# A channel's way back from its spectra, woven into the next channel's work (one Trainium2 core, four-block image network, channel stage)

## The chip, the cores and the metric

One core of one Trainium2 chip runs the whole program in one launch. The metric is device time in microseconds; lower is better. The kernel before took 14596.81 us (median of three runs, 14577.73 to 14602.56). Its profiled execution took 14588.21 us.

## What is computed

The reference applies four residual blocks to x (32 images, 192 channels, 56 x 56 pixels), each to a group-normalised input (32 groups of six channels):

```
x = x + L0(_gn(x), ...)    # agent attention
x = x + L1(_gn(x), ...)    # a recurrence over the pixels in both directions
x = x + L2(_gn(x), ...)    # every channel shifted by whole pixels, then blurred by 3 x 3 taps
x = x + L3(_gn(x), ...)    # a 55 x 55 convolution of every channel, by FFT
```

The last two are what the changed part computes. For L3:

```
xf = jnp.fft.rfft2(x, s)
kf = jnp.fft.rfft2(k[0], s)
y = jnp.fft.irfft2(xf * kf[None], s)
y = y[..., Kh // 2:Kh // 2 + H, Kw // 2:Kw // 2 + W]
return y + bias * x
```

The group norm between L2 and L3 needs the mean and the variance of six whole channels before any of the six can be convolved.

## The kernel before

The program has four stages in a row: `make_filter` (the filter's spectra), `attention` (L0), `scan_pairs` (L1) and `channel_blocks` (L2 and L3). Only `channel_blocks` is touched. It fills the last 30% of the span.

It works channel by channel, with all 32 images of a channel in one tile of 114 partitions (two images of 56 rows, each with a row of means) by 16 image pairs by 56 columns. Channels go in groups of GROUP = 6, which are the norm's groups. A group passes through these helpers:

- `shift(q, j)`, once for each channel. It loads x (L1477), multiplies it by a row matrix (16 TensorE instructions in two batches of PSUM, L1484; VectorE scales and evicts each to `turned`, L1491), then by a column matrix (L1501), adds the result to x (L1509) and sums x (L1510). `matrices` makes the two matrices for four channels at a time on GpSimd; one of them passes through TensorE (L1446) and VectorE (L1448).
- `middle(q)`: the group's mean, six small matmuls (L1517) and a copy (L1522).
- `centre(q, j)`, once for each channel: x less the mean into a padded tile (VectorE, L1526), its squares (ScalarE, L1528) and their sums (VectorE, L1529).
- `spread(q)`: 1 / sqrt of the variance, six matmuls (L1517) and two ScalarE instructions (L1534, L1535).
- `convolve(q, j)`, once for each channel, in five steps that depend on each other. **Row spectra**: 16 TensorE instructions (eight float32 matmuls, each recorded as two instructions) into three PSUM tiles (L1627), evicted by 12 ScalarE copies to `y` (L1633). **Column spectra**: for three batches of 5, 5 and 6 image pairs a real and an imaginary matmul (L1547, into the PSUM tiles `re` and `im`). **Products** with the filter's spectrum: six VectorE instructions a batch (L1554 to L1560), which leave `real` and `imag`. **Way back along one axis**: 32 matmuls (64 instructions, L1567) into four PSUM tiles, each evicted by ScalarE to `z` (L1574). **Way back along the other**: four matmuls (eight instructions, L1583) into two PSUM tiles, which VectorE scales (L1585) and adds to x (L1586). Two DMAs then store x (L1588).

The driving loop pairs the groups. While group n is shifted and centred, group n - 1 is convolved, one channel for each j: at j = 0, 1, 2 two channels of group n are shifted and one of group n - 1 convolved ("shift channels" below), at j = 3, 4, 5 two are centred and one convolved ("centre channels"). The first group has nothing to convolve beside it and the last nothing to shift.

What sets the order of instructions on an engine: the Tile framework's scheduler. It takes the program's order as the priority and moves an instruction ahead where its own model finds an earlier one not ready. Each engine then executes its list in that order, with semaphores between the engines. As built, each shift channel's TensorE list holds both shifts in full, then the row spectra, the column spectra and both ways back of one channel. Only the seams overlap: the first batches' way back (L1567) stands among the last batch's column spectra (L1547).

Pools: `d_x` has 15 tiles x, `d_w` two of each work tile (`y`, `real`, `imag`, `z`, `turned` and the rest). PSUM's eight banks are four `ps` tiles, two `re` and two `im`. The four `ps` tiles serve L1484, L1501, L1627, L1567, L1583, L1517 and L1446 alike.

Of the kernel before, what the change touches and what calls it, by code (L numbers as in the profile page):

```python
# [20 lines left out]
F32 = mybir.dt.float32  # L21
# [24 lines left out]
GROUP = C // 32  # L46
# [1314 lines left out]
def channel_blocks(ctx: ExitStack, tc: tile.TileContext, a, k, x2, rs2, spectra, out):  # L1361
# [10 lines left out]
    NI, NG = NB // 2, NB // 4  # L1372
# [3 lines left out]
    wp = ctx.enter_context(tc.tile_pool(name="d_w", bufs=2))  # L1376
# [51 lines left out]
    def matrices(n):  # L1428

        if n in made:  # L1430
            return made[n]
        got = []
        for d, diff in ((1, diff_y), (0, diff_x)):
            r, m = diff.shape
            t = [wp.tile([r, m], F32, name=f"tap{d}{f}", tag=f"tap{d}{f}", bufs=1) for f in range(3)]
            for f in range(3):
                i = 2 * n + d
                nc.gpsimd.tensor_scalar(
                    t[f], diff, where[:r, i, f : f + 1], gs[:r, i, f : f + 1], ALU.is_equal, ALU.mult
                )  # L1440
            mat = wp.tile([r, m], F32, name=f"mat{d}", tag=f"mat{d}", bufs=3)
            nc.gpsimd.tensor_tensor(t[0], t[0], t[1], ALU.add)
            nc.gpsimd.tensor_tensor(mat, t[0], t[2], ALU.add)
            if d == 1:
                ps = pp.tile([128, BANK], F32, name="ps", tag="ps", bufs=4)
                nc.tensor.matmul(ps[:PR, :PR], lags, mat, start=True, stop=True)  # L1446
                mat = wp.tile([r, m], F32, name="mat2", tag="mat2", bufs=3)
                nc.vector.tensor_copy(mat, ps[:PR, :PR])  # L1448
            got.append(mat)
        made.clear()  # L1450
        made[n] = got
        return got
# [18 lines left out]
        return q  # L1471

    def shift(q, j):
        c = q.n * GROUP + j
        rows, cols = matrices(c // 4)
        x = xp.tile([PR, NI, S], F32, name="x", tag="x")
        nc.sync.dma_start(out=x, in_=x2[c].rearrange("s h g w -> (s h) g w"))  # L1477
        flat = x.rearrange("p g w -> p (g w)")
        turned = wp.tile([2 * S, NG, 2, S + 1], F32, name="turned", tag="turned")
        for g0 in range(0, NG, 4):  # L1480
            n = min(4, NG - g0)
            ps = psum()
            for g in range(n):
                nc.tensor.matmul(  # L1484
                    ps[: 2 * S, g * PR : (g + 1) * PR],
                    flat[:, (g0 + g) * 2 * S : (g0 + g + 1) * 2 * S],
                    rows,
                    start=True,
                    stop=True,
                )  # L1490
            nc.vector.tensor_tensor(  # L1491
                turned[:, g0 : g0 + n].rearrange("p g s h -> p (g s) h"),
                ps[: 2 * S, : n * PR].rearrange("p (g h) -> p g h", h=S + 1),
                _bc(q.scale[:, j, g0 : g0 + n].rearrange("p g s -> p (g s)"), [2 * S, 2 * n, S + 1]),
                ALU.mult,
            )
        for g0 in range(0, NG, 4):
            n = min(4, NG - g0)
            ps = psum()
            for g in range(n):  # L1500
                nc.tensor.matmul(  # L1501
                    ps[:PR, g * 2 * S : (g + 1) * 2 * S],
                    turned[:, g0 + g].rearrange("p s h -> p (s h)"),
                    cols,
                    start=True,
                    stop=True,
                )
            xc = flat[:, g0 * 2 * S : (g0 + n) * 2 * S]
            nc.vector.tensor_tensor(xc, xc, ps[:PR, : n * 2 * S], ALU.add)  # L1509
        nc.vector.tensor_reduce(q.sums[:, 0, j, :], x, AX.X, ALU.add)  # L1510
        q.x.append(x)

    def means(q, i):

# [5 lines left out]
    def middle(q):  # L1520
        q.mean = sp.tile([PR, NI], F32, name="mean", tag="mean")
        nc.vector.tensor_copy(q.mean, means(q, 0))  # L1522

    def centre(q, j):
        t = padded[(q.n * GROUP + j) % len(padded)]
        nc.vector.tensor_tensor(t[:, :, 0:S], q.x[j], _bc(q.mean, [PR, NI, S]), ALU.subtract)  # L1526
        sq = wp.tile([PR, NI, S], F32, name="sq", tag="sq")
        nc.scalar.activation(sq, t[:, :, 0:S], AF.Square)  # L1528
        nc.vector.tensor_reduce(q.sums[:, 1, j, :], sq, AX.X, ALU.add)  # L1529
        q.padded.append(t)  # L1530
# [3 lines left out]
        nc.scalar.activation(q.rs, means(q, 1), AF.Ln, bias=eps)  # L1534
        nc.scalar.activation(q.rs, q.rs, AF.Exp, scale=-0.5)  # L1535

    def convolve(q, j):
        c = q.n * GROUP + j
        y = wp.tile([128, NI, 2, 42], F32, name="y", tag="y")
        _rows_to_spectra(nc, psum, q.padded[j], f1, y, NG)  # L1540
        real, imag = (wp.tile([84, NI, 2, 42], F32, name=n, tag=n) for n in ("real", "imag"))
        gr, gi = (q.g[:, j, i, :].unsqueeze(1) for i in range(2))
        for i0, n in _batches(NI):
            f = []
            for i, name in enumerate(("re", "im")):
                ps = pp.tile([84, BANK], F32, name=name, tag=name)
                nc.tensor.matmul(  # L1547
                    ps[:, : n * 84], f2[:, i, :], y[:, i0 : i0 + n].rearrange("p g s u -> p (g s u)"), start=True, stop=True
                )
                f.append(ps[:, : n * 84].rearrange("p (g u) -> p g u", u=42))  # L1550
            shape = [84, 2 * n, 42]
            a0, a1 = (wp.tile([84, 12, 42], F32, name=m, tag=m)[:, : 2 * n] for m in ("a0", "a1"))
            to = [t[:, i0 : i0 + n].rearrange("p g s u -> p (g s) u") for t in (real, imag)]
            nc.vector.tensor_tensor(a0, f[0], gr.to_broadcast(shape), ALU.mult)  # L1554
            nc.vector.tensor_tensor(a1, f[1], gi.to_broadcast(shape), ALU.mult)  # L1555
            nc.vector.tensor_tensor(to[0], a0, a1, ALU.subtract)  # L1556
            a0, a1 = (wp.tile([84, 12, 42], F32, name=m, tag=m)[:, : 2 * n] for m in ("a2", "a3"))
            nc.vector.tensor_tensor(a0, f[0], gi.to_broadcast(shape), ALU.mult)  # L1558
            nc.vector.tensor_tensor(a1, f[1], gr.to_broadcast(shape), ALU.mult)  # L1559
            nc.vector.tensor_tensor(to[1], a0, a1, ALU.add)  # L1560
        z = wp.tile([84, NI, 2, S], F32, name="z", tag="z")
        for i0 in range(0, NI, 4):
            n = min(4, NI - i0)
            ps = psum()
            for i in range(n):
                for m, part in enumerate((real, imag)):
                    nc.tensor.matmul(  # L1567
                        ps[:84, i * 2 * S : (i + 1) * 2 * S],
                        part[:, i0 + i].rearrange("p s u -> p (s u)"),
                        f3[:, m, :],  # L1570
                        start=(m == 0),
                        stop=(m == 1),
                    )
            nc.scalar.copy(  # L1574
                z[:, i0 : i0 + n].rearrange("p g m w -> p (g m w)"), ps[:84, : n * 2 * S]
            )
        x = q.x[j]
        for i0 in range(0, NI, 8):
            n = min(8, NI - i0)
            ps = psum()  # L1580
            got = ps[:PR, : n * S].rearrange("p (g w) -> p g w", w=S)
            for m in range(2):
                nc.tensor.matmul(got, f4[:, m, :], z[:, i0 : i0 + n, m, :], start=(m == 0), stop=(m == 1))  # L1583
            o = wp.tile([PR, 8, S], F32, name="o", tag="o")[:, :n]
            nc.vector.tensor_tensor(o, got, _bc(q.rs[:, i0 : i0 + n], [PR, n, S]), ALU.mult)  # L1585
            nc.vector.tensor_tensor(x[:, i0 : i0 + n], x[:, i0 : i0 + n], o, ALU.add)  # L1586
        for s in range(2):
            nc.sync.dma_start(  # L1588
                out=out[s::2, c].rearrange("b h w -> h b w"), in_=x[(S + 1) * s : (S + 1) * s + S]
            )  # L1590

    before = None
    for n in range(C // GROUP + 1):
        q = begin(n) if n < C // GROUP else None
        for j in range(GROUP):
            if q is not None:
                if j < 3:
                    shift(q, 2 * j)
                    shift(q, 2 * j + 1)
                else:  # L1600
                    if j == 3:
                        middle(q)
                    centre(q, 2 * j - 6)
                    centre(q, 2 * j - 5)
            if before is not None:
                convolve(before, j)
        if q is not None:
            spread(q)
        before = q


def _batches(n):
# [93 lines left out]
```

## Time and profile before

| | |
|---|---|
| median of three runs | 14596.81 us |
| profiled execution | 14588.21 us, of which the span is 14586.4 us |
| mean granted TensorE clock over the span | 0.927 |
| first store of the channel stage (L1588) | at 10065.4 us |
| the group means (L1522), 32 of them | from 10025.6 us to 14409.0 us |
| channel stage, 10127 to 14409 us (4282 us): TensorE busy | 3848.15 us, clock 0.98 |
| the same: VectorE busy | 3186.79 us |
| the same: ScalarE busy | 1284.45 us |

The page lists busy times, groups of instructions and DMA issues for the whole program. The channel stage has to be read from windows of the trace: the share of each engine there, the list of waits (engine and line, what it waited for, total, number, longest), and the timeline, in which each row is a start, a duration, an engine, a line, and in brackets the engine's idle time before it with what ended it.

### The profile page before, as it was taken

The numbers are of one execution on the slowest core, as the hardware profiler recorded it, in microseconds if no ns is written. First come the engines' busy times: TensorE is split into PE (matmuls) and PEld (weight loads), VectorE is DVE, ScalarE is ACT, GpSimd is POOL, SyncE is SP. The second block draws the span as 40 slices with busy tenths as digits, with TensorE's granted clock in tenths as the row PEclk, the third lists the DMA queues.
The fourth block names the chain that finished last, engine by engine and source line by source line (L and its number), as shares of the span: only waits on it lengthen the run. The fifth ranks groups of instructions, "written<-read, shape, count | busy, mean of one in ns | idle before, by whom it ended". The sixth has DMA issues, their size and how long they took to land. (4 is left out here: it accounts for less than half of the span.)

```text
span 14586.4 us, 164705 instructions
## 1 busy us (share of the span) xinstructions
PE 12276.2 (84%) x63542; PEld 7620.1 (52%) x63542; DVE 11320.3 (78%) x15929; ACT 5972.2 (41%) x10826; POOL 2178.7 (15%) x2238
## 2 busy tenths in 40 slices
PE   4999999999999976777677677767899889988898
PEld 2655655655565553333333333335666666666666
DVE  4878877887887878878887887886777777777777
ACT  2444444444444434444444444443323232323323
POOL 0000000000000004434443443442000000000000
PEclk8999999999999988888888888888999999999999
DMA  2001001000100112232223222322111111111111
GB/s 54 27 27 40 27 27 40 27 27 32 35 27 27 40 53 66 60 71 71 65 67 81 66 60 68 75 51 56 35 37 36 37 37 36 37 35 38 36 37 23
DMA packets 886784, 654.14 MB, mean 45 GB/s; under 512 B 764942, under 2 KB 772857, under 8 KB 876976
## 3 DMA queue, kind: packets, MB, share of 16 engines
q1 hardware_dynamic: 885992, 643.51, 16.7%
q8 instruction: 505, 8.27, 0.2%
q14 instruction: 287, 2.35, 0.1%
HBM read 402.88 MB, written 240.50 MB: 44 GB/s over the span
## 5 line engine op out<-in xcount | busy, mean ns | idle before, releaser
L587 DVE SCALAR_TENSOR_TENSOR o<-v_a,dww,o 128x896 f32<-128x896 f32 (+1 forms) x1024 | 1052.8, 1028 | 390.1 <-ACT v_a L561 282.7
L1633 ACT COPY y<-ps 64x252 f32<-64x252 f32 (+1 forms) x2376 | 807.6, 340 | 1298.6 <-PE ps L1627 1266.4
L1567 PE MATMUL ps<-f,imag 84*84 84x112 f32 x6144 | 1032.0, 261 | 130.2 <-DVE imag L1560 128.5
L1574 ACT COPY z<-ps 84x448 f32<-84x448 f32 x768 | 405.3, 528 | 1771.1 <-PE ps L1567 1771.1
L1567 PE MATMUL ps<-f,real 84*84 84x112 f32 x6144 | 1035.7, 261 | 1.7
L1567 PEld LDWEIGHTS ps<-f,imag 84*84 84x84 f32 x6144 | 744.0, 153 | 275.6 <-DVE imag L1560 206.4
L1567 PEld LDWEIGHTS ps<-f,real 84*84 84x84 f32 x6144 | 748.8, 153 | 160.1 <-issue 68.6
L1041 ACT ACTIVATE q<-q 128x784 f32<-128x784 f32 x384 | 329.3, 858 | 1225.4 <-DVE q L1036 1223.9
L1035 POOL COPY c<-p 128x1 f32<-128x1 f32 x384 | 696.2, 1813 | 665.3 <-DVE p L1034 611.8
L1048 POOL MEMSET c<- 128x1 f32 x192 | 18.3, 99 | 5182.8 <-PE ps L719 5172.1
L1034 DVE TENSOR_TENSOR_SCAN q<-decay,c,ek 128x784 f32<-128x784 f32 x384 | 702.0, 1832 | 105.3 <-ACT ek L1064 105.2
L1583 PE MATMUL ps<-z,f 84*114 84x448 f32 x1536 | 658.5, 551 | 129.5 <-ACT z L1574 129.5
L604 ACT ACTIVATE pr<-ps,low 98x896 f32<-98x896 f32 (+1 forms) x384 | 350.1, 914 | 1015.4 <-DVE low L602 1015.4
L1585 DVE TENSOR_TENSOR o<-ps,rs 114x448 f32<-114x448 f32 x384 | 239.5, 624 | 631.7 <-PE ps L1583 630.5
L1035 POOL COPY c<-q 128x1 f32<-128x1 f32 x384 | 483.1, 1258 | 1460.7 <-DVE q L1034 1390.3
L1034 DVE TENSOR_TENSOR_SCAN p<-decay,c,bv 128x784 f32<-128x784 f32 x384 | 699.9, 1833 | 0.0
L674 PE MATMUL ps<-gq_a,xs_a 128*112 128x294 f32 x1792 | 643.7, 442 | 0.0
L600 PE MATMUL ps<-xs_a,gk_a 128*98 128x448 f32 (+1 forms) x1536 | 639.0, 497 | 0.0
L587 DVE SCALAR_TENSOR_TENSOR o<-v_c,dww,o 128x448 f32<-128x448 f32 (+1 forms) x1024 | 634.0, 619 | 4.0
L1547 PE MATMUL re<-y,f 128*84 128x420 f32 (+1 forms) x1152 | 561.5, 569 | 84.8 <-ACT y L1633 74.8
L601 PE MATMUL ps<-xs_c,gk_c 125*98 125x448 f32 (+1 forms) x1536 | 631.6, 492 | 0.0
L675 PE MATMUL ps<-gq_c,xs_c 125*112 125x294 f32 x1792 | 627.7, 433 | 0.0
(352 smaller groups left out, 29243.6 us busy)
## 6 DMA issues: line engine op xcount, KB each, us to landing
x<-x SPq DMA_DIRECT2D x512, 392.0 KB
x<-x SPq DMA_DIRECT2D x512, 196.0 KB
x<-x SPq DMA_DIRECT2D x192, 399.0 KB
out_x<-x SPq DMA_DIRECT2D x384, 196.0 KB
x_a<-in_x SPq DMA_DIRECT2D x32, 1568.0 KB
x<-x_a SPq DMA_DIRECT2D x32, 1568.0 KB
x_c<-in_x SPq DMA_DIRECT2D x64, 392.0 KB
x<-x_c SPq DMA_DIRECT2D x64, 392.0 KB
```

The costliest lines, as they stand in the source:

```text
L587: nc.vector.scalar_tensor_tensor(dst, tap(i), dww[:, t, i : i + 1], dst, ALU.mult, ALU.add)
L600: mm(ps[P2, h, :n], g[:, cols], xs_a[j][:, px], start=True, stop=False)
L601: mm(ps[P2, h, :n], gk_c[0:KC, 2 * j + h, cols], xs_c[j][0:KC, px], start=False, stop=True)
L674: mm(ps[:SUB, i, :HA], xs_a[j][:, px], g, start=True, stop=False)
L675: mm(ps[:SUB, i, :HA], xs_c[j][0:KC, px], gq_c[0:KC, 2 * j + (q + i) // ns], start=False, stop=True)
L1034: nc.vector.tensor_tensor_scan(out, decay[:, of(t)].to_broadcast([128, MC]), data, at, ALU.mult, ALU.add)
L1035: nc.gpsimd.tensor_copy(at, s[:, last : last + 1])
L1547: nc.tensor.matmul(ps[:, : n * 84], f2[:, i, :], y[:, i0 : i0 + n].rearrange("p g s u -> p (g s u)"), start=True, stop=True)
L1567: nc.tensor.matmul(ps[:84, i * 2 * S : (i + 1) * 2 * S], part[:, i0 + i].rearrange("p s u -> p (s u)"), f3[:, m, :], start=(m == 0), stop= ...
L1574: nc.scalar.copy(z[:, i0 : i0 + n].rearrange("p g m w -> p (g m w)"), ps[:84, : n * 2 * S])
L1583: nc.tensor.matmul(got, f4[:, m, :], z[:, i0 : i0 + n, m, :], start=(m == 0), stop=(m == 1))
L1633: nc.scalar.copy(y[64 * m : 64 * m + 64, 2 * g0 + i : 2 * (g0 + n) : 2], got[64 * i : 64 * i + 64, :, :, m, :])
```

## The change

`convolve` is cut in two, and all helpers become generators that yield between steps. `analyse` holds the row spectra, the column spectra and the products; `synthesise` holds both ways back, the addition to x and the stores. The driving loop runs `synthesise` of a channel one turn later, beside the next channel's `analyse`, and takes the steps of four generators in turn: the analysis (`taking`), two shifts or centres (`two`), and the previous channel's way back (`ending`). `middle` moves into the first `centres`. No instruction is added, removed or changed in size; pools and tiles are the same.

```
-    def convolve(q, j):
-        c = q.n * GROUP + j
+    def analyse(q, j):
+
         y = wp.tile([128, NI, 2, 42], F32, name="y", tag="y")
         _rows_to_spectra(nc, psum, q.padded[j], f1, y, NG)
-        real, imag = (wp.tile([84, NI, 2, 42], F32, name=n, tag=n) for n in ("real", "imag"))
+        yield
+        real, imag = q.product = [wp.tile([84, NI, 2, 42], F32, name=n, tag=n) for n in ("real", "imag")]
...
             nc.vector.tensor_tensor(to[1], a0, a1, ALU.add)
+            yield
+
+    def synthesise(q, j, product):
+
+        c = q.n * GROUP + j
+        real, imag = product
         z = wp.tile([84, NI, 2, S], F32, name="z", tag="z")
...
+            yield
         x = q.x[j]
...
             nc.vector.tensor_tensor(x[:, i0 : i0 + n], x[:, i0 : i0 + n], o, ALU.add)
+            yield
...
-    before = None
+    def centres(q, j):
+
+        if j == 0:
+            middle(q)
+        centre(q, j)
+        yield
+        yield
+
+    before, ending = None, iter(())
     for n in range(C // GROUP + 1):
         q = begin(n) if n < C // GROUP else None
         for j in range(GROUP):
+            two = [iter(()), iter(())]
             if q is not None:
-                if j < 3:
-                    shift(q, 2 * j)
-                    shift(q, 2 * j + 1)
-                else:
-                    if j == 3:
-                        middle(q)
-                    centre(q, 2 * j - 6)
-                    centre(q, 2 * j - 5)
-            if before is not None:
-                convolve(before, j)
+                two = [shift(q, 2 * j + i) if j < 3 else centres(q, 2 * j - 6 + i) for i in range(2)]
+            taking = analyse(before, j) if before is not None else iter(())
+            for step in (
+                taking, two[0], two[0], taking, ending, ending, two[0], taking, ending, ending, two[1], two[1], taking,
+                ending, two[1], ending,
+            ):
+                next(step, None)
+            for rest in (*two, taking, ending):
+                for _ in rest:
+                    pass
+            ending = synthesise(before, j, before.product) if before is not None else iter(())
         if q is not None:
             spread(q)
         before = q
+    for _ in ending:
+        pass
```

`shift` yields after its row pass and after its column pass, and otherwise stays as it was. The scheduler still stands between this order and the chip. As built, TensorE's list for a shift channel c is: row spectra of c, row pass of one shift, column pass with the first column spectra of c among it, half the way back of c - 1 (L1567 before), the second column spectra, the other half, the second shift's two passes with the third column spectra among them, L1583 of c - 1. A centre channel has the same without the shifts.

More of the change, by code (lines that the diff above doesn't have):

```diff
@@ L1590, in convolve @@
             )
-    before = None
+    def centres(q, j):
+        if j == 0:
+            middle(q)
+        centre(q, j)
+        yield
+        yield
+    before, ending = None, iter(())
     for n in range(C // GROUP + 1):
```

## Prediction

> **What bounds the kernel now.** The page first: TensorE has the largest share of the whole span.
>
> ```profile
> PE 12276.2 (84%) x63542; PEld 7620.1 (52%) x63542; DVE 11320.3 (78%) x15929; ACT 5972.2 (41%) x10826; POOL 2178.7 (15%) x2238
> ```
>
> That is an average over four stages. The window from the group of means at 10127 us to the last mean at 14409 us is the changed stage alone (busy times in the order PE, PEld, DVE, ACT, POOL, then granted clock, DMA share, GB/s):
>
> ```profile
> 10127.00:14409.00 4282.00, 3848.15 (x24547) 2831.01 (x24546) 3186.79 (x5284) 1284.45 (x3105) 264.67 (x410) 0.98 0.14 36
> ```
>
> TensorE is busy 90%, VectorE 74%, ScalarE 30%, DMA 14%. So TensorE is the bound, with holes. Who makes the holes is in the waits of 10600 to 14586 us (total, times, longest):
>
> ```profile
> PE ps L1583 <- ACT z L1574: 113.9, 169, 1.0
> PE ps L1567 <- DVE imag L1560: 112.4, 168, 0.8
> PE ps L1501 <- DVE turned L1491: 73.8, 108, 0.8
> PE re L1547 <- ACT y L1633: 64.5, 178, 1.7
> PE ps L1484 <- DVE mat L1448: 23.7, 40, 0.7
> ```
>
> The first two are once a channel: TensorE runs through a channel's chain faster than VectorE's products and ScalarE's copies follow. How long TensorE's steps last when nothing holds them is in the timeline, from one start to the next:
>
> ```profile
> 12017.99 2.45 PE L1627 MATMUL ps<-f,padded 114*128 114x168 f32 x16
> 12020.59 0.94 PE L1547 MATMUL re<-y,f 128*84 128x420 f32 x2 [0.15 <-ACT y L1633]
> 12022.10 0.94 PE L1547 MATMUL re<-y,f 128*84 128x420 f32 x2
> 12023.58 1.01 PE L1547 MATMUL re<-y,f 128*84 128x504 f32 x2
> 12025.27 0.36 PE L1567 MATMUL ps<-f,real 84*84 84x112 f32 x2
> 12025.46 0.35 PE L1567 MATMUL ps<-f,imag 84*84 84x112 f32 x2
> 12028.33 0.42 PE L1567 MATMUL ps<-f,imag 84*84 84x112 f32 x2 [0.60 <-DVE imag L1560]
> 12030.56 1.67 PE L1583 MATMUL ps<-z,f 84*114 84x448 f32 x4
> 12034.76 1.76 PE L1583 MATMUL ps<-z,f 84*114 84x448 f32 x4 [0.62 <-ACT z L1574]
> 12040.99 1.74 PE L1484 MATMUL ps<-mat,x 114*112 114x114 f32 x16
> 12043.52 1.85 PE L1501 MATMUL ps<-mat,turned 112*114 112x112 f32 x16 [0.80 <-DVE turned L1491]
> 12045.21 2.46 PE L1627 MATMUL ps<-f,padded 114*128 114x168 f32 x16
> ```
>
> Column spectra (L1547) take 1.51 + 1.48 + 1.69 = 4.7 us, a pair on L1567 0.19 us, L1501 1.69 us. The durations shown hold the pipeline's tail (0.17 us in a pair of 0.36), so each listed wait costs about 0.17 us more than it says. A last view, the granted clock (last but two) in 4 us stretches around a mean:
>
> ```profile
> 12112.00:12116.00 4.00, 3.38 (x24) 2.48 (x23) 1.45 (x3) 1.06 (x2) 0.00 (x0) 1.00 0.00 0
> 12120.00:12124.00 4.00, 4.00 (x15) 3.55 (x14) 2.92 (x4) 3.03 (x7) 0.00 (x0) 0.50 0.50 100
> ```
>
> After the wait for z and the small L1517 matmuls TensorE runs some 5 us at half clock. Over the stage that is 0.98.
>
> **What the Trainium skill says.** "Perfetto Trace Analysis", section "Identifying the Most-Contended Engine": matmul busy time is a poor measure of how near TensorE is to its limit. The trace agrees: the means come every (14409.0 - 10025.6) / 31 = 141.4 us a group, and the streaming summed below is 119. "TensorE: Matmul & The Clock Gate", section "Part 1: The HAM clock gate": an idle window halves the clock; the 0.50 above agrees on the half, though here under 1 us of idle and some small matmuls were enough. The same page, "Architectural detail": ScalarE and VectorE are strict FIFOs, so the built order decides who blocks whom; the trace shows no instruction overtaking.
>
> **The change part by part.** A group is three shift channels (two shifts beside one convolution) and three centre channels. Nothing is added or removed in work, so I price TensorE's list and then what can still hold it.
>
> TensorE's streaming. Row spectra: (2.45 - 0.31) / 15 x 16 = 2.3 us (0.31 is one instruction). Column spectra 4.7. Way back on L1567: 32 pairs x 0.19 = 6.1. L1583: eight instructions at 0.375 = 3.0. Together 16.1 a channel. A shift: L1484 1.6, L1501 1.7, so 3.3, twice in a shift channel. Group: 6 x 16.1 + 6 x 3.3 = 116.2; the twelve mean matmuls 2 x 1.13 = 2.3; L1446 0.4. **118.9 us against 141.4 now.** VectorE, from its starts in the timeline: 12 products at 0.50 and 6 at 0.59 = 9.6, four L1585/L1586 at 0.6 = 2.4; two centres and their sums add 4.0, two shifts 6.6. So 16.0 in a centre channel and 18.6 in a shift channel, below TensorE's 16.1 and 22.7.
>
> Moved: the way back of channel c - 1 (L1567, L1574, L1583, L1585, L1586, the stores).
> - L1567's wait for imag: its operands are finished one channel earlier. VectorE ends the last imag of c - 1 about 2 us into c's turn; the half that needs it comes 8 us in. Waits nothing. Without that cover it is 0.60 + 0.17 again.
> - L1583's wait for z: 1.7 us of third column spectra lie between the last L1567 and L1583; z needs 0.3 + 0.53. Nothing.
> - L1501's wait for turned: in each built shift either one column-spectra matmul (0.75) stands before L1501, or only the second L1484 batch. I take 0.1 each, 6 x 0.1 = 0.6; bounds 0 and 0.80 + 0.17.
> - y: row spectra end at 2.3, the first four copies at 2.46, the next reader starts at 2.6. In centre channels it is the column spectra, in shift channels now L1484 or L1446, because the built order gives it the bank that those copies free. 0.31 a channel; the first centre channel hides it under L1517. 5 x 0.31 = 1.6.
> - L1484 behind the matrix copy L1448, which on VectorE now stands behind L1585: 1.5 a group, 0.2 each = 0.3.
>
> A wait the change adds: in the built list the third row-spectra bank of centre channels is the one L1583 of the channel before last filled. On VectorE its reader L1585 stands behind the third products, and these behind L1529, which waits for the square, which waits on ScalarE behind 12 copies y. Counting a centre channel from its first row-spectra matmul: products start at 3.6, y ends 5.3, square 6.2, L1529 7.3, second products 9.3 (ready 8.1), third products end at about 18.0, L1585 18.3. The third bank is wanted at 16.4 + 1.7 = 18.1. So about 0.4 once a group; behind it TensorE's whole list waits. Bounds 0 and 3 x 1.8 (rival B).
>
> On SP the stores now stand one channel later, ahead of the same load of x; a tile x is freed one channel later of 15. A load is issued some four channels (70 us) before its L1484, with DMA 14% busy: nothing.
>
> Clock: the idle before L1517 goes, so I take half of today's loss, 1.2 us a group (2% of 118.9 is 2.4; bounds 0 and 2.4).
>
> Sum: 118.9 + 0.6 + 1.6 + 0.3 + 0.4 + 1.2 = **123.0 us a group**, 18.4 less. 31 groups have a partner: 570. The last group's six channels alone (18.4 now, from row spectra to row spectra; 16.5 then) give 11, less about 1 for the last way back, which stands uncovered at the end: 10. Total 580. Profiled execution 14588.2 - 580 = 14008. The median lies 8.6 above the profiled time, below what can be told here; I take **14010**.
>
> **Rivals.** A (above): TensorE is fed; 13930 to 14110 for the small waits' bounds.
>
> B: VectorE becomes the bound in centre channels. For: 16.0 against 16.1 leaves no room, and L1529's wait (1.25) and five hand-offs of 0.2 lie in its FIFO: 16.0 + 1.25 + 1.0 = 18.3 instead of 16.5. Against: it can catch up in shift channels (4 us of room), and the bank limits only once. 3 x 1.8 = 5.4 a group: 128.4, 14588 - 13.0 x 31 - 10 = 14175. With the turned waits at 0.97 each as well (5.2): 133.6, 14336.
>
> C: fed without holes, clock 1.00: 118.9, 14588 - 22.5 x 31 - 10 = 13880.
>
> D, slower: a denser TensorE is granted less clock. From 10127 us on, 118.9 / clock + 2.9 must exceed 142.3 (0.2% above now), so clock below 0.853. The scan stage shows 0.83 to 0.85; at 0.83 the group is 146.2, the time 14588 + 4.8 x 31 = 14735. Against: that stage is the less busy one (72%), and attention, 93% busy, shows 0.97.
>
> E: the scheduler puts the old order back: 14597. The built order excludes most of it: L1567 of c - 1 stands inside c on TensorE throughout.
>
> **How the numbers follow.** A 0.62, B 0.18 (0.04 of it at 14336), C 0.13, D 0.04, E 0.03. The range reaches from C's edge, 13890, to just past B's first price, 14190; outside lie D, E, B's upper part and a little of C, some 0.15. Faster by over 0.2% (about what a measurement of this kernel can tell from no change): 0.94; within: 0.02; slower: 0.04.
>
> **What would show it.** Right: the waits of L1567 for imag and L1583 for z are gone, the means come every 123 us, TensorE's busy share of the stage is above 96%, clock 0.98 to 1.00. Wrong: waits of L1627 for L1585 or of L1501 for turned of several us a group (B), a clock below 0.95 (D), the old interval (E).

## The result and the profile after

The changed kernel takes 13910.62 us (median of four runs, 13893.86 to 13911.89) against 14593.24 us before: a ratio of 0.9529, 95% interval 0.9518 to 0.9541. In a later series it took 13911.32 us. The prediction was 14010, with a range of 13890 to 14190. The profiled execution took 13893.86 us with a span of 13892.0 us, 694.4 us less than the span before.

Where the 694 us lie is read from the starts of the group means (L1522 before, L1525 after). The first interval is a special one: the first group has nothing to convolve beside its centres. All others are alike.

| | before | after | saved |
|---|---|---|---|
| start of the stage (first VectorE instruction, L1388) | 9975.9 | 9967.1 | 8.8 (earlier stages, not the change) |
| from there to the first mean | 49.7 | 48.8 | 0.9 |
| first interval, to the second mean (10118.77; 10095.14) | 93.1 | 79.2 | 13.9 |
| 30 further intervals, to the last mean (14409.0; 13730.1) | 30 x 143.01 | 30 x 121.17 | 655.2 |
| last mean to the end | 177.4 | 161.9 | 15.5 |

The page shows TensorE's busy time 280 us lower (12276.2 us before) in a span 694 us shorter. Time at half clock counts as busy there, and so does the tail of a matmul's record ahead of a wait.

```profile
PE 11996.5 (86%) x63542; PEld 7557.7 (54%) x63542; DVE 11279.1 (81%) x15929; ACT 5974.6 (43%) x10826; POOL 2193.0 (16%) x2238
```

The stage alone, 10127 to 13700 us (columns as in the prediction):

```profile
10127.00:13700.00 3573.00, 3531.15 (x24175) 2727.31 (x24176) 3099.76 (x5206) 1272.37 (x3066) 272.77 (x410) 1.00 0.17 43
```

TensorE is busy 98.8% of it, where it was 90%, and its clock is 1.00, where it was 0.98. What it still waits for, in all of 10600 to 13850 us (26.8 groups):

```profile
PE ps L1653 <- DVE o L1596: 8.5, 27, 0.3
PE ps L1446 <- issue: 8.4, 39, 0.3
PE re L1551 <- ACT y L1659: 6.1, 30, 0.2
PE ps L1520 <- ACT y L1659: 5.3, 26, 0.2
PE ps L1485 <- ACT y L1659: 4.7, 26, 0.2
```

The old waits for z, imag, turned and the matrix have no row any more. (A delay as short as the tail of the row before, 0.17 us, gets no row; e7 finds one.) Two centre channels and the second half of a shift channel on TensorE (L1653 are the row spectra, L1551 the column spectra, L1594 the second way back, L1485 and L1503 a shift):

```profile
12021.61 1.74 PE L1485 MATMUL ps<-mat,x 114*112 114x114 f32 x16
12023.38 1.02 PE L1503 MATMUL ps<-mat,turned 112*114 112x112 f32 x8
12024.24 1.01 PE L1551 MATMUL re<-y,f 128*84 128x504 f32 x2
12025.09 0.96 PE L1503 MATMUL ps<-mat,turned 112*114 112x112 f32 x8
12025.88 1.01 PE L1551 MATMUL im<-y,f 128*84 128x504 f32 x2
...
12047.32 2.44 PE L1653 MATMUL ps<-f,padded 114*128 114x168 f32 x16
12049.97 0.94 PE L1551 MATMUL re<-y,f 128*84 128x420 f32 x2 [0.21 <-ACT y L1659]
12054.51 0.87 PE L1551 MATMUL re<-y,f 128*84 128x420 f32 x2
12055.22 0.87 PE L1551 MATMUL im<-y,f 128*84 128x420 f32 x2
12058.99 1.01 PE L1551 MATMUL re<-y,f 128*84 128x504 f32 x2
12060.68 3.17 PE L1594 MATMUL ps<-z,f 84*114 84x448 f32 x8
12063.69 1.88 PE L1653 MATMUL ps<-f,padded 114*128 114x168 f32 x12
12065.88 0.84 PE L1653 MATMUL ps<-f,padded 114*128 114x168 f32 x4 [0.31 <-DVE o L1596]
12080.22 1.28 PE L1520 MATMUL ps<-sums,ones_rows 114*114 114x16 f32 x12
```

A centre channel takes 16.37 us (12047.32 to 12063.69), and the next, with the predicted wait for L1596 in its third row-spectra bank, 16.53. That wait is there but costs little: the channel that has it no longer waits for y.

### The profile page after: what moved, and what is told of

The parts are those of the page before. It is cut to its first block, busy times and chain, and to the rows that moved or that the text cites. A ratio compares the mean times of both kernels' runs of the same rounds, so it can differ in the third digit from the quotient of the medians.

```text
span 13892.0 us, 165068 instructions
## 1 busy us (share of the span) xinstructions
PE 11996.5 (86%) x63542; PEld 7557.7 (54%) x63542; DVE 11279.1 (81%) x15929; ACT 5974.6 (43%) x10826; POOL 2193.0 (16%) x2238
## 5 line engine op out<-in xcount | busy, mean ns | idle before, releaser
L1577 PE MATMUL ps<-f,real 84*84 84x112 f32 x6144 | 1090.8, 259 | 0.0
L1577 PE MATMUL ps<-f,imag 84*84 84x112 f32 x6144 | 1089.4, 259 | 0.0
L1577 PEld LDWEIGHTS ps<-f,real 84*84 84x84 f32 x6144 | 783.8, 153 | 134.3 <-issue 95.8
L1577 PEld LDWEIGHTS ps<-f,imag 84*84 84x84 f32 x6144 | 763.7, 153 | 0.0
L1594 PE MATMUL ps<-z,f 84*114 84x448 f32 x1536 | 608.8, 539 | 0.0
L835 PE MATMUL ps<-y,cen_aa 128*128 128x392 f32 x512 | 276.4, 704 | 318.2 <-DVE y L1105 318.2
L1443 POOL TENSOR_TENSOR mat<-tap,tap 114x114 f32<-114x114 f32 x96 | 40.8, 425 | 3166.0 <-PE ps L1503 2313.1
```

The lines of the kernel that those rows point to most:

```text
L1577: nc.tensor.matmul(ps[:84, i * 2 * S : (i + 1) * 2 * S], part[:, i0 + i].rearrange("p s u -> p (s u)"), f3[:, m, :], start=(m == 0), stop= ...
```

## The experiments

Each kernel is judged by its time beside runs of the kernel before on the same chip, and by its steady interval: (last mean - second mean) / 30, from one profile. That interval leaves out the earlier stages, which move by up to 30 us between these profiles (first mean from 10015.9 to 10046.1 us). Before: 143.01; after: 121.17. The clock is the mean granted one from 10127 to 13700 us. The changed kernel was run again beside the last experiment:

> The changed kernel itself, once more beside e9_early_total. Both theories: 13911 us as before, 121.2 us a group.

Measured: 13911.32 us, a ratio of 0.9528 (0.9515 to 0.9541), and 121.18 us a group.

| kernel | us | ratio to before | us a group | clock |
|---|---|---|---|---|
| e1: delay alone | 14168.1 | 0.9706 (0.9690 to 0.9722) | 129.61 | 0.98 |
| e2: weave alone | 14418.12 | 0.9879 (0.9863 to 0.9896) | 137.38 | 0.95 |
| e6: delay alone, matrices earlier | 14062.81 | 0.9629 (0.9614 to 0.9643) | 125.96 | 1.00 |
| e3: change + one VectorE instruction | 13899.27 | 0.9523 (0.9507 to 0.9539) | 120.53 | 1.00 |
| e4: change, way back ahead of the column spectra | 13935.31 | 0.9550 (0.9534 to 0.9566) | 122.23 | 1.00 |
| e5: change, one mean matmul | 14052.75 | 0.9627 (0.9614 to 0.9640) | 125.61 | 0.98 |
| e7: change, both column spectra in the hand-off | 13873.21 | 0.9500 (0.9487 to 0.9513) | 119.95 | 1.00 |
| e8: e5 and e7 | 14016.88 | 0.9599 (0.9586 to 0.9612) | 124.17 | 0.98 |
| e9: e7, one mean matmul, sums added early | 13829.61 | 0.9469 (0.9456 to 0.9482) | 118.27 | 1.00 |

### e1: the delay alone

```
+            for rest in two:
+                for _ in rest:
+                    pass
-            for step in (
-                taking, two[0], two[0], taking, ending, ending, two[0], taking, ending, ending, two[1], two[1], taking,
-                ending, two[1], ending,
-            ):
+            for step in (taking, taking, ending, ending, taking, ending, ending, taking, ending, ending):
```

> The changed kernel, but the two shifts or centres of a turn run in full first, as before; only the previous channel's way back is woven into the analysis. My theory (the gain is the way back's one-channel delay, which lets the L1567 matmuls start without waiting for imag and the L1583 matmuls without waiting for z): of today's group interval of 119.8 us only the shifts' own holes come back (the old waits for turned and for the row matrix, about 97 us in 28 groups, plus 0.17 us of pipeline tail each: 4.4 us a group), so 124.2 us a group and about 14045 us; granted clock 1.00, since the idle time ahead of the mean matmuls stays closed. Rival (the weaving with the shifts is what fills TensorE): at least 130 us a group, 14220 us or more.

Measured: 129.61 us a group, so 13.4 of the 21.8 us that the change saves. My 124.2 was wrong, and the rival's bound (130) nearly met. TensorE's waits, 10600 to 13850 us (25.1 groups):

```profile
PE ps L1503 <- DVE turned L1492: 84.8, 101, 1.0
PE ps L1485 <- DVE mat L1448: 47.8, 24, 2.0
PE re L1551 <- ACT y L1659: 21.8, 125, 0.2
PE ps L1485 <- ACT rs L1538: 10.5, 13, 0.8
```

The waits for imag and z are gone, as the theory has it. But the wait for the matrix had 0.7 us at most before and has 2.0 now. VectorE's timeline shows why:

```profile
12033.30 1.14 DVE L1596 TENSOR_TENSOR o<-ps,rs 114x448 f32<-114x448 f32 x2
12034.36 1.15 DVE L1597 TENSOR_TENSOR x<-x,o 114x448 f32<-114x448 f32 x2
12035.43 0.27 DVE L1448 COPY mat<-ps 114x114 f32<-114x114 f32 x1
```

The matrix's copy stands behind the delayed additions to x. TensorE waits for it behind the one matmul that makes the matrix (L1446), and then runs at half clock (row pass 12035.75, and the granted clock, last but two, of the 4 us that follow):

```profile
12030.39 3.17 PE L1594 MATMUL ps<-z,f 84*114 84x448 f32 x8
12033.40 0.36 PE L1446 MATMUL ps<-mat,lags 114*114 114x114 f32 x2
12035.75 3.38 PE L1485 MATMUL ps<-mat,x 114*112 114x114 f32 x16 [1.99 <-DVE mat L1448]
```

```profile
12036.00:12040.00 4.00, 4.00 (x22) 4.00 (x23) 1.26 (x2) 0.00 (x0) 2.03 (x4) 0.50 0.50 100
```

19 of the 24 waits for the matrix are followed by half clock, and none of the 24 has a mean matmul in the 5 us before it. The wait for rs in the last row (13 times) does stand behind the twelve small mean matmuls and L1446; half clock follows 10 of these.

### e6: the delay alone, with the matrices made a turn earlier

```
         q.x.append(x)
+        if c % 4 == 1 and c // 4 + 1 < C // 4:
+            matrices(c // 4 + 1)
         yield
```

(`matrices` also keeps two sets, in the three buffers it had.)

> The kernel with the way back delayed by a channel but the shifts run in full first (e1_skew_alone), and in it the two shift matrices are made one turn earlier than they are needed. It tests why e1_skew_alone took 129.6 us a group and not 124.2. My theory now: with the delay alone the row matrix's copy on VectorE stands behind the previous channel's last additions to x, TensorE idles 2.0 us ahead of the row pass (1.5 times a group), and that idle beside the small mean matmuls brings some 5 us at half clock. Both go with earlier matrices: 3.0 us of wait and 2.4 us of clock off, about 124.5 us a group, granted clock 1.00, about 14010 us. Rival (the rest of the loss is the shifts' own holes, whatever the matrix): the wait goes but the interval falls by 2 us or less, 14110 us or more, and the clock stays at 0.98.

Measured: 125.96, that is 3.65 less than e1, and the clock is 1.00 again. So the waits ahead of the row pass (for the matrix and, 0.4 us a group, for rs) and the half clock behind them were what e1 lost beyond the shifts' own holes, and the rival (2 us or less, clock 0.98) falls. My 124.5 was 1.5 too low, and the matrix wait does not stand beside the mean matmuls, as I had put it. What is left of the list (10600 to 13850 us, 25.8 groups) is the shifts' own hand-off and y:

```profile
PE ps L1504 <- DVE turned L1493: 113.3, 128, 1.1
PE re L1554 <- ACT y L1662: 16.8, 92, 0.2
```

113.3 / 25.8 = 4.4 us a group, with 0.17 of tail for each of 128 waits 5.2. The changed kernel is 4.8 us a group faster than this one: about what the weave takes away once the delay works undisturbed. (That the two are the same 4.8 is a sum, not a run.)

### e2: the weave alone

```
+    def late(q, j):
+        yield from synthesise(q, j, q.product)
...
+            ending = late(before, j) if before is not None else iter(())
             for step in (
-                taking, two[0], two[0], taking, ending, ending, two[0], taking, ending, ending, two[1], two[1], taking,
-                ending, two[1], ending,
+                taking, two[0], two[0], taking, taking, two[0], ending, two[1], taking, ending, two[1], ending, two[1],
+                ending, ending, ending,
             ):
```

> The changed kernel, but a channel's way back runs in the same turn as its own analysis; the shifts are woven among the two. My theory: the centre channels have nothing to put into the waits for imag and z and keep their old 18.4 us (16.4 now) and the old first centre channel (22.8 against 17.6), the shift channels lose about half of their holes: 119.8 + 2 x 2 + 5.2 + about 3 = 132 us a group, some 14290 us, and the stretches at half clock around the means come back. Rival (weaving fills TensorE): 124 us or less a group, 14040 us or less.

Measured: 137.38, 5.6 less than before and 5.4 more than I expected. The rival (124 or less) falls clearly. TensorE's waits, 10600 to 13850 us (23.7 groups):

```profile
PE ps L1577 <- DVE real L1560: 77.9, 48, 1.6
PE ps L1577 <- DVE imag L1564: 59.5, 70, 1.1
PE ps L1594 <- ACT z L1584: 43.2, 70, 0.6
```

180.6 / 23.7 = 7.6 us a group are waits for the channel's own products and copies, which the delay removes, with 188 tails of 0.17 us another 1.3. The clock of 0.95 adds 5% of 118 = 5.9. That is 14.8 of the 16.2 us by which it trails the changed kernel. Shift work fills such waits only where there is shift work: from one channel's first row-spectra matmul to the next, the three shift channels take 69.8 us (69.6 in the changed kernel), the three centre channels 67.5 (51.6). Most of the half clock (24 of 30 stretches) lies in the first centre channel, not around the means, where I expected it. I also expected the shift channels to lose only half of their holes.

### e3: more work for VectorE

```
             nc.vector.tensor_tensor(to[1], a0, a1, ALU.add)
+            if i0 == 0:
+                more = wp.tile([PR, NI, S], F32, name="more", tag="more", bufs=1)
+                t = q.padded[j][:, :, 0:S]
+                nc.vector.tensor_tensor(more, t, t, ALU.add)
             yield
```

> The changed kernel with one more VectorE instruction a channel, after the first products: a 114 x 896 sum into a tile that nobody reads, about 1.0 us as L1526. It computes nothing that is used. If TensorE alone sets the pace (my theory): the shift channels absorb it, the centre channels, where VectorE has 16.0 us of work against TensorE's 16.4, lengthen by up to 0.6 us: 0 to 2 us a group, 13910 to 13975 us. If VectorE is the bound (rival B of the prediction): 6 us a group, about 14095 us.

Measured: 120.53. The added instructions are there (VectorE busy 3278.59 us of 3573, 3099.76 without them) and cost nothing (I had allowed for up to 2 us a group):

```profile
10127.00:13700.00 3573.00, 3533.02 (x24275) 2733.77 (x24274) 3278.59 (x5416) 1282.31 (x3087) 277.82 (x410) 1.00 0.17 43
```

So VectorE at 87% is not the bound; the prediction's rival B falls. The 0.64 us a group that it gained come with another built order: between the two passes of a shift the scheduler put one or both column-spectra matmuls in 117 of 156 shifts (10600 to 13850 us), and in only 52 in the changed kernel. e7 tests that order by itself.

### e4: the way back ahead of the column spectra

```
-                taking, two[0], two[0], taking, ending, ending, two[0], taking, ending, ending, two[1], two[1], taking,
+                taking, ending, two[0], two[0], taking, ending, two[0], taking, ending, ending, two[1], two[1], taking,
```

> The changed kernel with one step of the weave moved: the first quarter of the previous channel's way back (eight L1567 pairs, 1.5 us) stands between the row spectra and whatever follows them. If the 0.36 us between the row spectra and the next reader of y or of its bank is what is left to gain (my theory), it goes in all six channels of a group: 2 us a group, about 13850 us. Rival: TensorE already streams without holes that count, or the products start 1.5 us later and VectorE, late, holds the third row-spectra bank longer: 13910 us or more.

Measured: 122.23, 1.1 more. The hole was not filled but moved (10600 to 13850 us):

```profile
PE ps L1653 <- ACT y L1659: 40.7, 54, 1.1
PE ps L1577 <- ACT y L1659: 13.6, 71, 0.2
```

The third row-spectra matmuls now wait up to 1.1 us for copies of y, and the L1577 matmuls too: the four `ps` banks are handed out anew, and what follows the row spectra needs a bank that only those copies free. My theory (the hole behind the row spectra can be had by this reordering) falls for the steady groups. In the last group, which has no shifts or centres beside it, a channel does get shorter, from 16.38 to 15.94 us. The rival's cause, VectorE holding that bank, isn't what the list shows either.

### e5 and e8: one matmul for the mean and for the variance

```
-        for j in range(GROUP):
-            nc.tensor.matmul(ps[:PR, :NI], ones, q.sums[:, i, j, :], start=(j == 0), stop=(j == GROUP - 1))
+        one = sp.tile([PR, NI], F32, name=f"one{i}", tag=f"one{i}")
+        nc.vector.tensor_reduce(one, q.sums[:, i].rearrange("p j i -> p i j"), AX.X, ALU.add)
+        nc.tensor.matmul(ps[:PR, :NI], ones, one, start=True, stop=True)
```

> The changed kernel, but the six channels' sums are first added on VectorE (one small reduction) and the group's mean and variance take one matmul each in place of six. If TensorE's own streaming is what bounds the stage now (my theory), the ten small matmuls that go, 20 recorded instructions of 1.13 us / 12 = 0.094 us, come off in full: 1.9 us of 121.2 us a group (interval of the means after the first two), so 119.3 us and about 13850 us. Rival (hand-offs between the engines set the interval): the one matmul still has to wait for the sum and its hand-off takes the place, 0.5 us a group or less, 13895 us or more.

> One mean matmul (e5_one_mean) and the swapped steps (e7_spectra_between) together on the changed kernel. If both remove TensorE time and nothing else is near its limit, they add up: 3.1 us a group, about 13815 us. Rival (VectorE, at 87% of the stage, becomes the bound): no more than the larger of the two alone, 13850 us or more.

Measured: e5 125.61, a loss of 4.4 where I expected a gain of 1.9. e8 124.17, or 14016.88 us where I expected 13815: it keeps e5's loss, with a gain like e7's on top (1.4). First VectorE, then TensorE at the end of a group of e5:

```profile
12047.59 0.61 DVE L1598 TENSOR_TENSOR x<-x,o 114x448 f32<-114x448 f32 x1
12048.13 0.61 DVE L1597 TENSOR_TENSOR o<-ps,rs 114x448 f32<-114x448 f32 x1
12048.66 0.30 DVE L1520 TENSOR_REDUCE one<-sums 114x16 f32<-114x96 f32 x1
```

```profile
12043.64 1.67 PE L1595 MATMUL ps<-z,f 84*114 84x448 f32 x4
12049.11 0.54 PE L1521 MATMUL ps<-one,ones_rows 114*114 114x16 f32 x2 [3.80 <-DVE one L1520]
12049.48 4.83 PE L1654 MATMUL ps<-f,padded 114*128 114x168 f32 x16
```

VectorE stood 4 us behind TensorE at that point. It does so in the changed kernel too: there the last L1596 of this turn starts at 12083.20, when TensorE has been through with L1594 for 3 us. It costs nothing because TensorE asks for nothing that late. The new reduction sits at the end of VectorE's list, and TensorE does ask for it. The row spectra after it (16 instructions in 4.83 us, 2.44 otherwise) run at half clock. 3.8 + 0.17 of wait and 2% of 118 for the clock (0.98), less the 1.9 that went: 4.4, as measured. e5's rival had this cause right, that the one matmul waits for its sum, though not its size. The amount of VectorE work, e8's rival, is not the cause: e9 has the same reductions and none of the loss.

### e7: both column-spectra matmuls in the hand-off

```
-                taking, two[0], two[0], taking, ending, ending, two[0], taking, ending, ending, two[1], two[1], taking,
-                ending, two[1], ending,
+                taking, two[0], taking, two[0], ending, ending, two[0], taking, ending, ending, two[1], taking, two[1],
+                ending, two[1], ending,
```

> The changed kernel with two steps of the weave swapped in each half of a shift turn, so that both column-spectra matmuls of a batch (1.5 us) stand between a shift's row pass and its column pass, in place of one between the column pass's halves. In the changed kernel the column pass starts 0.2 us after the row pass ends, six times a group. If that hand-off (VectorE's turned, which is the column pass's stationary operand) is a hole, it is covered: 1.2 us a group, about 13875 us. Rival: it is TensorE's own cost of a change of operand and comes back in the new place: 13905 us or more.

Measured: 119.95 and 13873.21 us: 1.22 us a group, the size expected, but not from six hand-offs. The changed kernel has them in only 104 of its 156 shifts (10600 to 13850 us), 3.9 a group. There the column pass starts 1.77 us after the row pass and its first half takes 0.86 us, its second 0.80. In the other 52 a column-spectra matmul already stands between the passes; from start to start, the row pass takes 1.57 us here and the column pass 1.59:

```profile
12085.75 1.74 PE L1485 MATMUL ps<-mat,x 114*112 114x114 f32 x16
12087.32 0.87 PE L1551 MATMUL re<-y,f 128*84 128x420 f32 x2
12088.03 1.76 PE L1503 MATMUL ps<-mat,turned 112*114 112x112 f32 x16
12089.62 0.36 PE L1577 MATMUL ps<-f,real 84*84 84x112 f32 x2
```

That is 0.25 us for each hand-off, 1.0 us a group, and the three shift channels lose just this (69.56 to 68.55 us). The delay was a hand-off of `turned`, which the column pass reads, and not a fixed cost of TensorE. The other 0.2 us is the third bank's wait for L1596: it has no row in e7's list, and the last centre channel takes 17.45 us for 17.65. Part of the agreement with my 1.2 us is therefore luck.

### e9: the sums added where they are made

On e7, one matmul for each mean, with the reduction called directly behind the sixth channel's sum:

```
         nc.vector.tensor_reduce(q.sums[:, 1, j, :], sq, AX.X, ALU.add)
+        if j == GROUP - 1:
+            total(q, 1)
```

(The same behind the sums of x; `total` is e5's reduction.)

> The swapped steps (e7_spectra_between) and one matmul for the mean and for the variance, with the six channels' sums added on VectorE directly behind the last of them, not at the end of the turn as in e5_one_mean and e8_both. If e5_one_mean was slow only because that small reduction stood at the end of VectorE's list, some 4 us behind TensorE, and its wait then halved the clock: the wait goes, 1.9 us a group come off the 119.95 of e7_spectra_between, 118.1 us a group and about 13815 us, clock 1.00. Rival (one matmul behind a chain of sums is late wherever it stands): 122 us a group or more, 13940 us or more.

Measured: 118.27 and 13829.61 us, the fastest version: 0.9469 of before (0.9456 to 0.9482). The wait for the reduction has no row in its list, and the clock is 1.00. Of the 1.9 us a group that TensorE no longer has to do, 1.7 come off the time. The other 0.2 is the third bank's wait, which e7 had lost and which is back in e9's list (8.6 us, 27 times).

## Why the prediction was right, and where its sizes were off

- **TensorE with holes is the bound**: shown. Added VectorE work costs nothing (e3), TensorE work taken away comes off almost whole where no new wait takes its place (e9 against e7; e5 is the other case).
- **Waits for imag and z**: gone, as priced. e1 and e6 have the delay and no such waits; e2 has no delay and keeps them. Delay and undisturbed matrices are 143.01 - 125.96 = 17.0 of the 21.8 us. Earlier matrices without the delay were not run; the kernel before waits 23.7 us in 28 groups for the matrix, from which I estimate their share at some 1 us of the 17.
- **Waits for turned**: priced at 0.1 in each of six shifts, 0.6 a group. They are 0.25 in 3.9 of them and nothing in the rest, 1.0 a group (e7). A shift with the wait takes 1.77 + 0.86 + 0.80 = 3.4, one without it 3.2, where I had summed 3.3 + 0.1.
- **y and the third bank**: both there at nearly the size forecast (row spectra to next start 2.65 against 2.6; L1596 at 12065.22, which is 17.9 us after its turn's first row spectra, against 18.3). But they don't add: the bank's wait replaces that for y. And the first centre channel, which I thought hid its wait for y under the mean matmuls, has it (L1520 in the list above), so that five such waits a group came out right for the wrong reason.
- **Column spectra** were sized at 4.7 a channel from the kernel before, where they followed a wait. Running freely they take 0.71 each in batches of five and 0.85 in that of six: 4.53. 1.0 us a group.
- **Clock**: I took half of the loss away; all of it went (1.00). 1.2 us a group. e1 shows that the delay alone would not have done it.
- **The base**, "the means come every (14409.0 - 10025.6) / 31 = 141.4 us a group", was the term that failed most. The mean over 31 intervals holds the short first one (93.1). A steady group takes 143.01, so each of 30 was worth 1.6 more. (In the other base, the list, 6 x 16.1 + 6 x 3.3 is 116.4 and not 116.2.)
- The sum again: 30 x (143.01 - 121.17) = 655.2 against 31 x 18.4 = 570; with the first interval (13.9), the end (15.5 against 10), and 9.7 ahead of the first mean, nearly all from the earlier stages, 694 against 580. The errors mostly point the same way. The median lies inside the range by 21 us only, because its edge was set at C's price.
- **Rivals**: B falls (e3), D and E are excluded by the clock and the vanished waits. C, TensorE fed without holes, is nearest in time: 13910.62 us against its 13880, and 121.2 a group against its 118.9. With the column spectra at their true size its sum is 117.9; of the 3.3 between, some 2.4 lie in and behind the row spectra (the waits for y and for the third bank) and 1.0 in the hand-offs of turned.

## What to carry to other kernels

When the busiest engine's holes are waits inside one item's dependent chain, run the second half of the chain one item later: the delay does what filling with unrelated work can't, because it also works where there is no unrelated work. Then look at what the move pushes back in the other engines' FIFOs (here a matrix copy, a small reduction): an engine may lag by several microseconds for free until the bound engine asks for something at the end of its list. And count a periodic stage by its steady intervals alone.

## What the hardware showed unexpectedly

A hole can cost more than its length: after some waits, the traces show 3.4 us or more at a granted clock of 0.50.

| run | wait | how many are followed by half clock |
|---|---|---|
| before | 0.6 us for z, then twelve mean matmuls of 16 columns | 20 of 46 |
| before | 1.7 us for y, ahead of column spectra | 0 of 13 |
| e1 | 2.0 us for the matrix, behind L1446 alone | 19 of 24 |
| e1 | 0.8 us for rs, behind twelve mean matmuls and L1446 | 10 of 13 |
| e2 | 1.6 us for real, behind other waits in the first centre channel | 24 of 24 |
| e2 | 1.6 us for real, behind column spectra | 0 of 24 |
| e5 | 3.8 us for the reduction, ahead of one mean matmul | 26 of 26 |
| e6 | 0.8 to 1.1 us for turned | 0 of 128 |

(All from 10600 to 13850 us.) Over that stretch the clock is 0.98 in the kernel before, e1 and e5, 0.95 in e2, and 1.00 wherever such waits are gone. The length of the wait alone doesn't decide: 0.6 us beside mean matmuls can be enough, and 1.7 us elsewhere was not. What does decide, no run here separates.
